# The second attention's edge list in rows of eight tiles, each with one span of 128 nodes

## The chip, the core and the metric

The kernel runs on one core of a Trainium2 chip. The time is the device time of one launch in microseconds (us), median of the runs shown. Names used below: PE is TensorE (matmuls; PEld its weight loads), DVE is VectorE, ACT is ScalarE, POOL is GpSimd, which here issues the gathers, SP is the engine whose queue starts most other transfers. SBUF is the on-chip memory, PSUM the small memory in eight banks that PE writes its products to.

## What is computed

A graph of 6250 nodes with 256 features goes through four steps, each added to its input: a graph attention over 206,250 edges, a mixture of eight experts, a weighted sum over the edges, and a second attention over another list of 131,072 edges, whose result picks two of four experts per node. The change is about the second attention. Cut to what matters:

```python
def second(x, src, dst):                   # x: 6250 x 256, 131072 edges
    h = (x @ W_gat).reshape(M, 4, 4)       # 4 heads, 4 experts
    e = leaky_relu(a_src[src] + a_dst[dst], 0.2)     # a_src, a_dst: sums of h * att
    ee = exp(e - segment_max(e, dst)[dst])
    alpha = ee / (segment_sum(ee, dst)[dst] + 1e-16)
    agg = segment_sum(h[src] * alpha[:, :, None], dst).reshape(M, 16) + b_gat
    scores = layernorm(agg).reshape(M, 4, 4).mean(1)
    topk_s, topk_i = top_k(scores, 2)
    w = softmax(topk_s)
    out = sum over e of where(topk_i == e, w, 0).sum(-1) * (gelu(x @ W1[e] + b1[e]) @ W2[e] + b2[e])
    return x + out
```

(A loop edge from each node to itself is part of both attentions; the kernel adds it apart from the lists.)

## The kernel before

One program, four stages, one after the other: the first attention (0 to about 2700 us), the experts with the sort of the second edge list beside them (to about 3700), the weighted sum (to about 6255), and the second attention (to the end of the span).

**Streams.** Both attentions run over an edge list sorted by destination, cut into *tiles* of 128 edges. A `Stream` (class at line 963) says which nodes a tile may meet. The destination of an edge at position p is close to p divided by the mean number of edges per node (`ratio`, 16 for the second list); `slack` is the largest deviation of ratio x destination from the position that the plan allows, and a check at run time (`check_stream`) chooses between the fast path described here and a slow one. Without groups (the second list, `s1`, line 1972), `window(b)` gives for each block b of 128 nodes the tiles that can hold edges into it: 16 tiles and 5 on each side for the slack of 640, so neighbouring windows overlap by ten tiles. With groups (the first list, `s0`, groups of 16 tiles), each group gets one *span* of 128 nodes that holds all that its tiles can meet. Spans don't begin at multiples of 128; `parts_of(b)` lists the spans that touch block b. `windows(t0, n)` lists the windows or spans that the tiles t0 to t0+n-1 meet.

**The loop.** `gat_stream` (1191 to 1449) does an attention. It works on *pieces* of Q = 8 tiles, in *batches* of B = 32 tiles (four pieces). The second list has 787 tiles, 99 pieces. The order of instructions on every engine is written out by hand (`manual_schedule`, the loop from 1405): engines take their queues strictly in this order, and step s_ issues

- `gathers(s_)`: eight indirect DMAs on POOL (1260) that fetch the source rows into `g` (nine buffers; the buffer of piece p comes free when `messages(p - 9)` of DVE is done),
- `load(s_+2)` on SP: `db` (destinations, 1244), once per batch `kf` (1253), and for a grouped stream `nbw`, the node part of one span (1249),
- `scores(s_-2)`: `node_parts` on PE multiplies the turned one-hot matrix `ot` of each tile by the node part (1281), into the PSUM tile `pd`; DVE sums its three terms (`nd`, 1290) and makes the scores (`z`, `Z`, 1292 to 1296); ACT copies edges of `Z` (1298, 1300),
- `move_sums` (grouped streams only, 1389): see below,
- `turned_hots(s_-1)` on DVE: `ot` (1270), one instruction for each window that the piece meets,
- `sums(s_-7)` on PE, the first two tiles (1363), and once per batch `turn_scores` (PE 1306, `zt`) and `greatest` (DVE scans `R`, `M`, 1312 and 1315),
- `one_hots(s_-6)` on DVE: `oh` (1152), one instruction for each window, comparing `ips` (node numbers, in PSUM) with the destinations,
- the rest of `sums`, which adds oh x messages to `acc`, one PSUM accumulator for each window,
- once per batch `turn_back` (PE 1323 and 1324, ACT exponentials 1328 and 1332, DVE products with `il` 1333),
- `keep_sums` (grouped only, ACT 1376), `done` for blocks whose sums are complete (in the second attention the DVE row `a` at 1781 and what follows it),
- `messages(s_-6)` on DVE: scaling (1340) and, in the second attention, splitting into three bf16 terms (1345, 1347).

`beside()` is called several times per step and issues other work: in the second attention first what is left of the second experts (PE 1714 and 1725, ACT 1719 and 1730, whose `y_d` stores go through SP), later the weighted additions to X (DVE 1813).

Without groups, `acc` of window b is already the sum of block b. With groups, `keep_sums` copies the finished sum of a span from PSUM to SBUF (`kept`), and in the next step `move_sums` adds it into the blocks that it touches (`bacc`), by a matmul with an identity matrix read at an offset (`shift_to`, `wide`).

PSUM: `place_iota` puts `ips` into a bank of its own, and `pd` has another. The node part in three bf16 terms, `NB`, stays in SBUF for an ungrouped stream; for a grouped one it is written to DRAM once (1221) and read back per span.

Of the kernel before, what the change touches and what calls it, by code (L numbers as in the profile page):

```python
# [20 lines left out]
F32 = mybir.dt.float32  # L21
# [11 lines left out]
P = 128  # L33
# [2 lines left out]
CH = 7  # L36
PAD = 30000
SLACK0 = 1024
SLACK1 = 640
GROUP0 = 16  # L40


def n_tiles(edges, nt):
# [28 lines left out]
def tile_kernel(ctx, tc, src_ins, out):  # L72
# [592 lines left out]
    I = src_ins  # L665
# [294 lines left out]
    Q = 8  # L960
# [172 lines left out]

    B = 32

    def place_iota(pp):

        t = pp.tile([P, 2 * P], F32, name="ips")
        nc.scalar.copy(t[:, :P], iota)
        nc.vector.tensor_scalar(t[:, P:], iota, float(P), None, op0=OP.add)  # L1140
        return t
# [49 lines left out]
    def gat_stream(s, H, CD, si, il, dl, tab, NI, early, done, parts=1, beside=None, pe=None):  # L1191
# [8 lines left out]
        W = DH + 2 * H  # L1200
        T = s.T
        ND = 2 * H
# [3 lines left out]
        with ExitStack() as st:  # L1206
# [5 lines left out]
            with tc.tile_pool(name="split", bufs=1) as sp:  # L1212
                NB = (sp if s.group else gp).tile([P, NT, 3, ND], BF, name="NB")
# [7 lines left out]
                    nc.sync.dma_start(nb_d.rearrange("(t p) d -> p t d", p=P), NB.rearrange("p t s d -> p t (s d)"))  # L1221
            mp = pool("gw", 2)
            pp = pool("gp", 1, space=PSUM)
            ips = place_iota(pp)
            piece, Z, acc, turned, hots, dbs, kfs, ps, ended = {}, {}, {}, {}, {}, {}, {}, {}, []
            items, split = {}, {}
            beside = beside or (lambda: False)

            def span(q):
                return q * Q, min(Q, T - q * Q)  # L1230
# [42 lines left out]

            def node_parts(q):
                t0, n = span(q)
                pd = pp.tile([P, Q, 3, ND], F32, name="pd", bufs=1)
                bl = turned.pop(q)
                for j in range(n):
                    use = [(b, o, t0 + j - a) for b, a, m, o in bl if a <= t0 + j < a + m]
                    for k, (b, o, i) in enumerate(use):  # L1280
                        nc.tensor.matmul(pd[:, j].rearrange("p s d -> p (s d)"), o[:, i * P:(i + 1) * P],
                                         nbw[b] if s.group else NB[:, b].rearrange("p s d -> p (s d)"),
                                         start=(k == 0), stop=(k == len(use) - 1))
                return pd
# [24 lines left out]
            def greatest(i, zt):  # L1309
                kf = kfs.pop(i)  # L1310
                R = mp.tile([P, 3 * P], F32, name="R")
                nc.vector.tensor_tensor_scan(R, kf[:, :3 * P], zt.rearrange("p k e -> p (k e)"), 0.0,  # L1312
                                             op0=OP.mult, op1=OP.max)
                M = mp.tile([P, 2 * P], F32, name="M")
                nc.vector.tensor_tensor_scan(M[:, ::-1], kf[:, 3 * P:P:-1], R[:, 3 * P - 1:P - 1:-1], 0.0,
                                             op0=OP.mult, op1=OP.max)
                d = mp.tile([P, P], F32, name="d")
                nc.vector.tensor_sub(d, zt[:, 1], M[:, :P])
                return d, M
# [51 lines left out]
            def keep_sums():  # L1371

                while ended:
                    i = ended.pop(0)
                    t = mp.tile([P, W], F32, name="kept", bufs=2)
                    nc.scalar.copy(t, acc.pop(i).rearrange("p s w -> p (s w)"))
                    moved.append((i, t))

# [16 lines left out]
            with tc.manual_schedule():  # L1395
# [9 lines left out]
                while s_ < last or later:  # L1405
# [10 lines left out]
                    if 0 <= k < npiece:  # L1416
                        scores(k, node_parts(k))
# [8 lines left out]
                    if batch:  # L1426
                        zt = turn_scores(i)
                        d, M = greatest(i, zt)
# [8 lines left out]
                    if s.group:  # L1437
                        keep_sums()
                        while ready:
                            b = ready.pop(0)  # L1440
                            follow(done(b, sums_of.pop(b), items.pop(b), mp))
# [9 lines left out]
    NB = 13  # L1451
# [293 lines left out]
    def layer1_fast(s1, si, dl1, il1, HN, tab_1, y_d, rest):  # L1745
# [4 lines left out]
        with tc.tile_pool(name="g1f", bufs=1) as g1, tc.tile_pool(name="f1w", bufs=2) as fp:  # L1750
# [75 lines left out]
            def beside():  # L1826
                if not rest() and work:
                    work.pop(0)()
                return bool(work)

            gat_stream(s1, H1, C1, si, il, dl, tab_1, NI, early, done, parts=3, beside=beside)

    moves = {}

    def fast(flag_s0, last_d, dl_d):
# [11 lines left out]
        with tc.tile_pool(name="gat0f", bufs=1) as g0:  # L1847
# [4 lines left out]
            with tc.tile_pool(name="rows", bufs=1) as p:  # L1852
                sr = load_rows(p, I["src"], s0.edges, C, I32, "sr")
                sf = p.tile([P, C, P], F32, name="sf")
                t = p.tile([P, C, P], F32, name="tt")
# [109 lines left out]
            with tc.tile_pool(name="f0h", bufs=1) as hp, tc.tile_pool(name="mix_ps", bufs=1, space=PSUM) as xp:  # L1965
                mix = xp.tile([P, 4 * P], F32, name="mix")
                par = head.params(hp)
                gat_stream(s0, H0, C0, si, il, dl, tab, NI, early, done, beside=lambda: next(par, True) is None,
                           pe=mix[:, :P].rearrange("p (b h) -> p b h", h=H0))


        s1 = Stream("s1", I["L1_ffn_edge_index"].shape[1], SLACK1, 1 << NB)
        C1s = s1.C
        si1 = dram.tile([P, C1s * P], I32, name="si1")
        dl1 = dram.tile([P, C1s * P], F32, name="dl1")
# [214 lines left out]
    for a, b in x_rows(x_in):  # L2190
        nc.scalar.dma_start(b, a)
    s0 = Stream("s0", I["src"].shape[0], SLACK0, N, GROUP0, True)
    last_d = dram.tile([P, s0.C, P], F32, name="last_d")
# [4 lines left out]
    with tc.If(v == 1) as cmp:  # L2198
        fast(s0, last_d, dl_d)
# [25 lines left out]
```

## Time and profile before

| what | value |
|---|---|
| three runs | 7765.84, 7773.18, 7774.26 us; median 7773.18 |
| profiled execution | 7783.37 us, its span 7781.5 us |
| granted PE clock, mean of the span | 0.717 |
| busy in the span | DVE 57%, POOL 53%, PE 49%, PEld 37%, ACT 15% |

By stage, busy us of each engine:

| stretch, us | PE | PEld | DVE | ACT | POOL | clock |
|---|---|---|---|---|---|---|
| 0 to 2700 | 1341.84 | 1034.21 | 1404.18 | 329.47 | 1544.64 | 0.73 |
| 2700 to 3700 | 876.16 | 756.89 | 470.24 | 250.03 | 252.15 | 0.94 |
| 3700 to 6255 | 1343.84 | 905.36 | 1705.19 | 471.84 | 1537.45 | 0.73 |
| 6255 to 7782 | 265.22 | 204.71 | 885.31 | 109.77 | 761.83 | 0.53 |

How to read what follows. A row of instructions gives the line, the engine, the operation, the output and inputs by their names in the program, the sizes (partitions x elements), the count, then busy us and mean ns of one, then the engine's idle time just before them and what ended most of it. A row of the timeline begins with its start and its duration in us; in brackets stands how long the engine had been idle before it and what released it. "remote" there is a release that the profile can't put down to a row, "issue" a time in which the engine waited for nothing that the profile shows. The ends of matmuls are modelled from their issue. Releasers are inferred.

### The profile page before, as it was taken

To read this page: it belongs to the slowest core of one execution; us is meant where nothing else is said; L and a number is where in the kernel's file an instruction comes from. 1 tells how busy PE (TensorE), PEld (TensorE's weight loads), DVE (VectorE), ACT (ScalarE), POOL (GpSimd) and SP (SyncE) were. 2 spreads that over 40 slices of the span, in tenths; PEclk is the share of its full clock that TensorE was granted. 3 is DMA by queue.
4 is the path that set the end of the run, shared out by engine and by line. 5 is a ranking of instruction groups with operands and counts; after the bars stand their busy time and mean duration, and the time that the engine had idled before them with its cause. 6 is when DMAs were issued, how large, how long until landed. Compare 5 with 4: busy or idle time off the path is not lost. (4 is left out here: it accounts for less than half of the span.)

```text
span 7781.5 us, 62325 instructions
## 1 busy us (share of the span) xinstructions
PE 3827.1 (49%) x17463; PEld 2901.2 (37%) x17463; DVE 4464.9 (57%) x10655; ACT 1161.1 (15%) x2758; POOL 4096.1 (53%) x4320
## 2 busy tenths in 40 slices
PE   3345545555445599996135555655555651111111
PEld 2234434444334378885023333433343431111111
DVE  4345555555555673443566666776676615665666
ACT  2011111111111112321001222212221210000000
POOL 0666666666666322321566666666566445555552
PEclk9667777777777799998557777777777875555555
DMA  4444444444444245565433333333333212222221
GB/s 124 119 114 119 113 117 120 117 119 118 115 114 120 73 163 190 184 228 167 139 89 99 98 103 100 101 102 102 95 100 101 80 43 52 45 48 52 50 50 41
DMA packets 496232, 821.82 MB, mean 106 GB/s; under 512 B 143344, under 2 KB 315587, under 8 KB 495842
## 3 DMA queue, kind: packets, MB, share of 16 engines
q0 software_dynamic: 190880, 462.26, 22.4%
q1 hardware_dynamic: 292326, 343.79, 14.5%
q10 hardware_dynamic: 12668, 11.68, 0.5%
q8 instruction: 141, 2.31, 0.1%
q14 instruction: 217, 1.78, 0.1%
HBM read 743.27 MB, written 77.29 MB: 105 GB/s over the span
## 5 line engine op out<-in xcount | busy, mean ns | idle before, releaser
L234 POOL DMA_INDIRECT g<-tab_ef,si x1616 | 1537.3, 951 | 995.4 <-issue 557.9
L1260 POOL DMA_INDIRECT g<-tab,si x1612 | 1539.6, 955 | 924.5 <-issue 577.4
L2028 DVE SCALAR_TENSOR_TENSOR run<-g,wab,run 128x256 f32<-128x256 f32 x2626 | 1264.9, 488 | 551.0 <-remote 179.2
L1260 POOL DMA_INDIRECT g<-tab_1f,si1s x787 | 761.8, 968 | 666.3 <-issue 587.1
L1363 PE MATMUL acc<-g,oh 128*128 128x264 f32 x3224 | 981.8, 465 | 174.6 <-issue 105.7
L1363 PEld LDWEIGHTS acc<-g,oh 128*128 128x128 f32 x3224 | 747.6, 238 | 365.0 <-issue 127.7
L1290 DVE TENSOR_REDUCE nd<-pd 128x64 f32<-128x192 f32 (+1 forms) x301 | 105.8, 352 | 1138.1 <-remote 914.2
L1714 PE MATMUL pf<-xt,w 128*128 128x512 f32 (+1 forms) x832 | 479.7, 715 | 474.9 <-issue 163.3
L2142 PE MATMUL acc<-run,oh 128*128 128x256 f32 x808 | 295.2, 500 | 628.3 <-DVE oh L2032 261.6
L1725 PE MATMUL pf<-w,h 128*128 128x256 f32 x1568 | 410.6, 412 | 183.1 <-ACT y L1730 80.9
L2142 PEld LDWEIGHTS acc<-run,oh 128*128 128x128 f32 x808 | 192.9, 251 | 730.4 <-issue 444.8
L1340 DVE TENSOR_TENSOR g<-g,mix 128x2048 f32<-128x2048 f32 x202 | 457.5, 2265 | 0.0
L1714 PEld LDWEIGHTS pf<-xt,w 128*128 128x128 f32 x832 | 179.7, 235 | 665.2 <-issue 321.6
L1363 PE MATMUL acc<-s,oh 128*128 128x72 bf16 x1267 | 96.6, 251 | 665.9 <-DVE s L1345 491.1
L1725 PEld LDWEIGHTS pf<-w,h 128*128 128x128 f32 x1568 | 316.3, 207 | 253.4 <-ACT y L1730 87.4
L1306 PE MATMUL zt<-ident,Z 128*128 128x128 f32 x228 | 76.6, 400 | 676.7 <-issue 380.2
L630 PE MATMUL ph<-xe,w 128*128 128x256 f32 x1792 | 405.4, 383 | 4.7 <-DVE xe L618 4.7
L643 PE MATMUL py<-w,h 128*128 128x256 f32 x1792 | 397.3, 379 | 0.0
L630 PEld LDWEIGHTS ph<-xe,w 128*128 128x128 f32 x1792 | 341.2, 192 | 51.4 <-DVE xe L618 5.7
L643 PEld LDWEIGHTS py<-w,h 128*128 128x128 f32 x1792 | 335.6, 190 | 43.1
L1363 PEld LDWEIGHTS <-oh 128*128 128x128 bf16 x1267 | 90.2, 133 | 669.9 <-issue 576.9
L606 POOL DMA_INDIRECT xg<-tab_x,gi x112 | 125.8, 1123 | 387.6 <-PE pt L615 313.1
(506 smaller groups left out, 5933.3 us busy)
## 6 DMA issues: line engine op xcount, KB each, us to landing
w<-in_L_ffn_W SPq DMA_DIRECT2D x112, 1024.0 KB
db<-s_d SPq DMA_DIRECT2D x299, 256.0 KB
g<-tab_ef,si POOLq DMA_INDIRECT x1616
g<-tab,si POOLq DMA_INDIRECT x1612
y_d<-y SPq DMA_DIRECT2D x196, 128.0 KB
yb<-y_d SPq DMA_DIRECT2D x49, 512.0 KB
g<-tab_1f,si1s POOLq DMA_INDIRECT x787
yy<-tab_y SPq DMA_DIRECT2D x7, 1792.0 KB
```

The costliest lines, as they stand in the source:

```text
L234: nc.gpsimd.indirect_dma_start(out=dst, out_offset=None, in_=table, in_offset=bass.IndirectOffsetOnAxis(ap=si[:, t:t + 1], axis=0))
L606: nc.gpsimd.indirect_dma_start(out=xg[:, i, :], out_offset=None, in_=tab_x, in_offset=bass.IndirectOffsetOnAxis(ap=gi[:, 2 * j + i:2 * j + ...
L630: nc.tensor.matmul(ph, w1[:, k, f * P:(f + 1) * P], xe[:, k, :], start=(k == 0), stop=(k == KD - 1))
L643: nc.tensor.matmul(py, hs[f][:, i * P:(i + 1) * P], w2[:, f, :], start=(f == 0), stop=(f == FC - 1))
L1260: nc.gpsimd.indirect_dma_start(out=g[:, j, :DH + H], out_offset=None, in_=tab, in_offset=bass.IndirectOffsetOnAxis(ap=si[:, t0 + j:t0 + j ...
L1290: nc.vector.tensor_reduce(nd[:, :n], pd[:, :n].rearrange("p j s d -> p j d s"), AX.X, OP.add)
L1340: nc.vector.tensor_mul(gh, gh, ps[0][:, o:o + n, :, None].to_broadcast([P, n, H, CD]))
L1363: nc.tensor.matmul(acc[b].rearrange("p s w -> p (s w)"), oh[:, t - a], m_, start=(t == lo), stop=(t == hi))
L1714: nc.tensor.matmul(ph[:, :n], w1[:, e, k, f * P:(f + 1) * P], xts[g][:, k, :n], start=(k == 0), stop=(k == KD - 1))
L1725: nc.tensor.matmul(py[:, :D], hs[g, e, f][:, j * P:(j + 1) * P], w2[:, e, f, :], start=(f == 0), stop=(f == FC - 1))
L2028: nc.vector.scalar_tensor_tensor(at[:, i] if j < Q - 1 else r[i], g[:, j, :], w, at[:, i], op0=OP.mult, op1=OP.add)
L2142: nc.tensor.matmul(acc[i], oh[:, k], r[k], start=(q % 2 == 0 and k == 0), stop=(last and k == 1))
```

## The change

The second list is made a grouped stream with groups of eight tiles, and its slack goes from 640 to 496. A group is then one piece: 1024 edges, 64 nodes by the ratio, and 62 more for the slack on both sides, within one span of 128. Spans of neighbouring pieces begin 64 nodes apart. So:

- every piece meets one span; `ot` and `oh` are made once per piece, and each of its tiles has one weight load and matmul in `pd` and one in `acc`;
- the list has 786 tiles, 99 pieces as before;
- `NB` of the second attention is held only for a while, written to DRAM, and read back per span (`nbw`);
- the sums of a span are copied by ACT (`kept`, now `parts * W` = 72 wide in the second attention, W = 264 as before in the first) and added to the blocks by the shifted identity; a block is put together from four spans.

In `gat_stream`, which both attentions run, `ips` and `pd` come to lie in one PSUM tile of one bank, `bank`.

```diff
-SLACK1 = 640
+SLACK1 = 496
 GROUP0 = 16
+GROUP1 = 8
...
-    def place_iota(pp):
-
-        t = pp.tile([P, 2 * P], F32, name="ips")
+    def place_iota(t):
+
         nc.scalar.copy(t[:, :P], iota)
         nc.vector.tensor_scalar(t[:, P:], iota, float(P), None, op0=OP.add)
         return t
...
             pp = pool("gp", 1, space=PSUM)
-            ips = place_iota(pp)
+
+            bank = pp.tile([P, 4 * P], F32, name="bank", bufs=1)
+            ips = place_iota(bank[:, :2 * P])
+            pd = bank[:, 2 * P:2 * P + Q * 3 * ND].rearrange("p (j s d) -> p j s d", j=Q, s=3)
...
             def node_parts(q):
                 t0, n = span(q)
-                pd = pp.tile([P, Q, 3, ND], F32, name="pd", bufs=1)
                 bl = turned.pop(q)
...
                 while ended:
                     i = ended.pop(0)
-                    t = mp.tile([P, W], F32, name="kept", bufs=2)
+                    t = mp.tile([P, parts * W], F32, name="kept", bufs=2)
                     nc.scalar.copy(t, acc.pop(i).rearrange("p s w -> p (s w)"))
                     moved.append((i, t))
...
-        s1 = Stream("s1", I["L1_ffn_edge_index"].shape[1], SLACK1, 1 << NB)
+        s1 = Stream("s1", I["L1_ffn_edge_index"].shape[1], SLACK1, 1 << NB, GROUP1)
```

## The prediction, made before the changed kernel was run

> **What bounds the kernel now.** The change acts on one stage, the second attention, which begins with its first gathers at about 6261 us and runs to the end of the span. I read the slices first: from slice 33 on PE falls to 1 tenth, while DVE stands at 6 and POOL at 5, so no engine is full. Then busy time per stretch, in columns PE, PEld, DVE, ACT, POOL, granted clock, DMA share, GB/s:
>
> ```profile
> 6520.00:6636.00 116.00, 15.58 (x218) 12.48 (x218) 71.84 (x217) 6.81 (x22) 61.35 (x64) 0.50 0.20 49
> 6868.00:6984.00 116.00, 15.58 (x218) 12.47 (x218) 71.66 (x216) 6.81 (x22) 62.07 (x64) 0.50 0.21 49
> 7448.00:7564.00 116.00, 15.58 (x218) 12.49 (x218) 73.71 (x220) 6.81 (x22) 63.90 (x66) 0.50 0.21 49
> ```
>
> All stretches from 6404 to 7680 look so: 64 gathers (eight pieces) in close to 115.5 us (64 gathers began between 6856.06 and 6971.5), 14.4 us per piece. Is it POOL? A gather is 0.95 us and the next follows after 0.30, so 64 need 80 us. POOL has 35 us of slack per eight pieces; its waits are buffers that come back late. DVE's busy 72 us are 78 with the roughly 30 ns between its 216 instructions. The other 37.8 us are waits, by the groups of 6856 to 6971.5: nd 21.2, R 10.4, the il product 6.2. What do they wait for?
>
> ```profile
> 6901.85 0.65 PEld L1281 LDWEIGHTS <-ot 128*128 128x128 bf16 x13
> 6902.06 0.54 PE L1281 MATMUL pd<-NB,ot 128*128 128x24 bf16 x13
> 6902.42 0.10 PEld L1363 LDWEIGHTS <-oh 128*128 128x128 bf16 x1
> ...
> 6910.24 0.94 PE L1363 MATMUL acc<-s,oh 128*128 128x72 bf16 x13 [7.63 <-DVE s L1345]
> ...
> 6925.41 0.36 DVE L1290 TENSOR_REDUCE nd<-pd 128x64 f32<-128x192 f32 x1 [15.22 <-remote]
> 6925.81 0.19 DVE L1292 TENSOR_TENSOR z<-g,nd 128x32 f32<-128x32 f32 x1
> ...
> 6926.81 0.20 PE L1281 MATMUL pd<-NB,ot 128*128 128x24 bf16 x1 [15.63 <-DVE ot L1270]
> 6927.07 1.95 DVE L1152 TENSOR_TENSOR oh<-ips,dl1s 128x1024 bf16<-128x1024 f32 x2
> ...
> 6932.95 0.95 POOL L1260 DMA_INDIRECT g<-tab_1f,si1s  x1 [10.98 <-issue]
> ```
>
> nd reads only pd. z, the first reader of the gathered rows, then starts without a wait, so the 15.22 us were not for a gather. The matmuls of pd are listed (with modelled ends) at 6902, yet the reader starts 23 us later: at such places PE delivers late. The same is seen at 7591.50 (pd listed) and 7614.12 (nd, 15.08). It comes about once per batch of four pieces; in the first attention too, whose pieces already meet one window (nd at 1535.88, 8.75). Its cause is in no view I have. So the stage is bound by DVE's work in series with late deliveries of PE.
>
> **The change, part by part.** 787 tiles are 99 pieces; today a piece meets two windows, 8 + 5 tiles.
>
> ```profile
> L1152 DVE TENSOR_TENSOR oh<-ips,dl1s 128x1024 bf16<-128x1024 f32 x98 | 118.8, 1212 | 0.0
> L1152 DVE TENSOR_TENSOR oh<-ips,dl1s 128x640 bf16<-128x640 f32 x96 | 77.8, 811 | 0.0
> L1270 DVE TENSOR_SCALAR ot<-db,s_nid 128x1024 bf16<-128x1024 int16 x98 | 48.2, 491 | 4.3 <-DMA db<-s_d 4.3
> L1270 DVE TENSOR_SCALAR ot<-db,s_nid 128x640 bf16<-128x640 int16 x96 | 38.9, 405 | 0.0
> L1281 PE MATMUL pd<-NB,ot 128*128 128x24 bf16 x1267 | 63.1, 184 | 270.7 <-DVE ot L1270 214.7 <-issue 38.6 <-remote 14.8
> L1363 PE MATMUL acc<-s,oh 128*128 128x72 bf16 x1267 | 96.6, 251 | 665.9 <-DVE s L1345 491.1 <-DVE g L1347 95.3 <-issue 79.5
> ```
>
> *DVE, removed:* the second of each pair, 96 x (811 + 405 ns) = 116.7 us of busy time. Pairs overlap in part: by starts, two oh take 1.86 us (6927.07 to 6928.93) against 1.13 for one in the first attention (1507.44 to 1508.57), two ot about 0.78 against 0.46. That is 1.05 us per piece, 8.4 per eight; nothing lies over it.
>
> *PE, removed:* 5 of 13 pairs of weight load and matmul per piece in pd and in acc. When PE is on time this is worth nothing (15.6 of 116 us busy). When it is late it counts: 23.3 us for 13 pairs of pd would be 14.3 for 8. DVE then has 8.1 - 1.05 = 7 us of work over it, so that wait falls from 15.2 to about 7.3. A batch also has a smaller wait at R, behind the 13 sums; sums fall to 8, but two shift matmuls join them. Two batches: 2 x 7.9 less at nd, and 10.4 x 3/13 = 2.4 at R, 18 together. The bounds: nothing, if lateness is a fixed stretch of time that only slides, and 18. I take 10, nearer the middle because the first attention, with 8 pairs, still shows such waits (80.7 us at nd in 500 us).
>
> *PE and ACT, added:* each of 49 blocks is put together from 4 spans, 196 fp32 shift matmuls. The row of the same line in the first attention has 647 ns (264 wide), the 128-wide fp32 transposition 447; for 72 columns I take 0.4 us, 2 x 0.4 per piece on an engine that idles 100 of 116 us: nothing, and 13 us over the stage per 0.13 us that would show. ACT copies 99 sums (379 ns at 264 wide) beside 6.8 us of busy per 116: nothing. If that copy waits for late sums, Z's copies queue behind it on ACT, and turn_scores behind those, but PE itself is then the cause. The block's first DVE row, a, read acc straight after its sums; now it reads bacc, filled earlier in the step, and follows one step later. Only the last step of the stage is longer for it: +3 us.
>
> *SP, added:* NB goes to DRAM once and returns as 99 rows of 48-byte lines, 0.38 us of issue each on a queue with one db per piece: hidden, two pieces ahead. At the start it is not: the first nbw load must await NB's write (issued 177.8 in the first attention, first nbw at 189.6, so 12 us), and behind it in SP's queue stand db, kf and the FFN's y stores, whose landing lets ACT go on. Between 0 and 15 us; until 6404 the FFN's rest sets the pace anyway (POOL waits 53.5 us for ACT y), so what delays it counts: +10.
>
> *Slack 640 to 496, one tile fewer:* one gather, 1.25 us, in POOL's slack. The span of a piece is 64 nodes and 2 x 496/16 = 62 for the slack, so it fits 128. In the inputs 16 x destination minus position in the sorted list lies between -345 and 39, so the fast branch holds.
>
> *One bank for ips and pd, in both attentions.* By the trace, pd of the next piece runs inside oh: matmuls from 6926.81 and 6927.20, oh from 6927.07 to 6929. The Trainium skill, "PSUM — Partial Sum Buffer", section "PSUM bank collisions raise a hardware error", says that two engines may not use one bank on the same partitions at once, disjoint columns included, and that semaphores must guard it "by bank × quadrant (by bank is the simple version), not by address". This rule speaks against the change: by address pd stays where the row has it and costs 0; by bank it moves behind oh, and with no cover that is oh's 1.2 us at each of 301 pieces of both attentions, 361 us. No row here shows two engines on one bank. Cover is there: after oh come the messages (L1340 0.28 + 3 x 0.28 + 2 x 0.36 = 1.8 us here, one of 2.27 us in the first attention), and eight pairs of pd need 0.35 (1510.87 there, already behind oh). So on-time steps pay nothing; where PE is late it starts up to 1.2 us later, about 25 batches here: between 0 and 30, and I take +8.
>
> **The sum.** A period of eight pieces: 115.5 - 8.4 - 10 = 97, 12.1 us per piece. The first attention, with one window per piece, has 333 gathers in 500 us, 12.0 per piece, which agrees. Over 1274 us (6404 to 7678): 1274 x 18.4/115.5 = 203. Less 10 (start), 8 (bank), 3 (end): 182. The profiled execution is 7783.37 us (span 7781.5), 0.13% over the median of the runs, 7773.18; it would become 7601, the median 7591. What is late next: still PE's deliveries; POOL (80 of 97) comes close.
>
> **Rivals.**
> (1) *Only DVE's work goes*; the lateness is a fixed time per batch, or the shift matmuls fill what the pairs leave. For it: the first attention shows as much of it with 8 pairs. Against: fewer pairs lie ahead of nd. 1274 x 8.4/115.5 = 93, less 21: 72, giving 7701.
> (2) *POOL becomes the bound.* The lateness hangs on the second window and vanishes: 82 us per eight pieces, 1274 x 33.5/115.5 = 370, less 21: 7424. Against it: the first attention.
> (3) *Slower: the bank order is exposed.* pd must wait for oh and DVE for pd, in 301 pieces: 7591 + 361 = 7952 if never covered. It decides from 182/301 = 0.6 us per piece, when PE reaches pd more than 1.8 us after oh's end, as it may in the first attention, where PE is half busy with sums. Against: there pd follows the sums today already.
> (4) *The change doesn't act* (slow branch): excluded by the inputs.
>
> **Chances.** Forecast 0.55, its own range 7540 to 7650; rival 1 0.20; rival 2 0.08; rival 3 0.12; costs that just cancel the gain 0.05. A difference below 0.2% (15.5 us) can't be told from none. Faster: 0.55 + 0.20 + 0.08 = 0.83; within 0.05; slower 0.12. The range 7500 to 7715 takes in the forecast with its open costs (stall 0 to 18, start, bank) and rival 1, and leaves out rivals 2 and 3.
>
> **What would show it.** oh and ot once per piece, 1.21 and 0.49 us; pd and acc x786; 64 gathers in about 97 us; nd waits below 21 per eight pieces. If nd and R still wait 31, rival 1; if POOL shows no waits for buffers, rival 2. If in the first attention nd waits for pd just after each oh, and that stage is longer than before, the bank order costs. A wait of nbw for NB's write shows at 6260 to 6290.

## The result and the profile after

The changed kernel takes 7820.91 us (16 runs, 7781.04 to 7856.26) where the kernel before takes 7773.72 (16 runs, 7754.3 to 7796.24): ratio 1.005, interval 1.0035 to 1.0065. It is slower by half a percent. The profiled execution took 7818.24 us, its span 7816.4.

What the change removes is gone, by the groups of the second attention in the changed kernel (same columns as before):

```profile
L1152 DVE TENSOR_TENSOR oh<-bank,dl1s 128x1024 bf16<-128x1024 f32 x98 | 118.9, 1213 | 0.0
L1391 PE MATMUL bacc<-kept,wide 128*128 128x72 f32 x390 | 109.3, 434 | 384.8 <-ACT kept L1378 255.5 <-issue 123.1 <-ACT g L1334 6.0
L1365 PE MATMUL acc<-s,oh 128*128 128x72 bf16 x786 | 68.9, 250 | 248.6 <-DVE s L1347 230.3 <-issue 18.3
L1273 DVE TENSOR_SCALAR ot<-db,s_nid 128x1024 bf16<-128x1024 int16 x98 | 47.0, 480 | 14.8 <-DMA db<-s_d 14.8
L1283 PE MATMUL bank<-nbw,ot 128*128 128x24 bf16 x786 | 36.4, 181 | 415.9 <-DVE oh L1152 364.6 <-issue 48.3 <-DMA kf<-s_keep 1.5
L1292 DVE TENSOR_REDUCE nd<-bank 128x64 f32<-128x192 f32 x98 | 34.6, 353 | 639.5 <-remote 598.9 <-PE bank L1283 35.2 <-issue 4.7
```

oh and ot run once per piece, pd and acc have 786 matmuls. A shift matmul leaves two records here, so there are 390 (of 392) where I wrote 196. And nd now waits 639.5 us in the stage, against 372.6 before. Busy time by stretch, in the changed kernel:

```profile
6868.00:6984.00 116.00, 19.27 (x170) 15.62 (x170) 63.03 (x199) 8.14 (x30) 58.41 (x62) 0.50 0.22 49
7448.00:7564.00 116.00, 18.64 (x162) 15.12 (x163) 62.92 (x199) 8.14 (x30) 58.43 (x62) 0.50 0.23 49
```

DVE works 63 us of 116 where it worked 72, yet POOL now issues fewer gathers in the same time (62, not 64). So DVE's saved time became waiting. To compare kernels I take from each trace the time from the 13th to the 93rd nd of the second attention, a tenth of which is the mean of eight pieces, and DVE's gaps of over 0.3 us in it. The stage is counted from its first row on DVE (NI1f, at 6255.55 before and at 6239.66 after):

| | before | after |
|---|---|---|
| eight pieces, us | 114.9 | 117.3 |
| DVE's gaps in them, us | 37.1 | 46.5 |
| first row of the stage to its first nd, us | 104.8 | 117.9 |
| the same to the 13th nd, us | 238.1 | 261.0 |
| 93rd nd to the end, us | 138.3 | 142.7 |
| whole second attention, us | 1525.7 | 1576.6 |

The mean depends a little on where the 80 pieces begin: from the 9th to the 18th nd it is 113.0 to 115.8 us before and 117.3 to 120.4 after. The waits have also moved. Between 6400 and 7680, R waited 78.6 us and the il product 60.4 before, 9.8 and 4.3 after, while nd went from 247.9 to 494.6: nearly all of DVE's waiting now stands at nd.

The timeline of the changed kernel shows where nd waits (cut to the gathers that begin after a stop of POOL, to nd's long waits, and to PE and ACT around the first of them):

```profile
6913.77 0.94 POOL L1263 DMA_INDIRECT g<-tab_1f,si1s  x1 [10.42 <-issue]
...
6925.58 0.36 PE L1283 MATMUL bank<-nbw,ot 128*128 128x24 bf16 x8 [1.83 <-DVE oh L1152]
...
6935.07 0.22 ACT L1378 COPY kept<-acc 128x72 f32<-128x72 f32 x1 [14.98 <-remote]
...
6947.65 0.36 DVE L1292 TENSOR_REDUCE nd<-bank 128x64 f32<-128x192 f32 x1 [20.12 <-remote]
...
6954.10 0.94 POOL L1263 DMA_INDIRECT g<-tab_1f,si1s  x1 [10.49 <-issue]
...
6999.19 0.36 DVE L1292 TENSOR_REDUCE nd<-bank 128x64 f32<-128x192 f32 x1 [20.82 <-remote]
...
7012.54 0.98 POOL L1263 DMA_INDIRECT g<-tab_1f,si1s  x1 [18.65 <-issue]
```

pd is listed at 6925.58 and arrives 22 us later; kept, a copy on idle ACT, waits for late sums in the same stretch. What I had not asked of the trace before is what POOL does then. It issues gathers in unbroken rows, one each 1.25 us: here 24 from 6913.77 to 6943.7, and 32 from 6954.10 to 6993.9. Each wait of nd of 20 us lies in such a row, begins 13 us or more after its start, and ends 3 to 5 us after the end of its last gather. The kernel before has a similar picture. Its stops of POOL:

```profile
6856.06 1.03 POOL L1260 DMA_INDIRECT g<-tab_1f,si1s  x1 [8.98 <-issue]
...
6869.92 0.99 POOL L1260 DMA_INDIRECT g<-tab_1f,si1s  x1 [4.06 <-issue]
...
6891.54 1.04 POOL L1260 DMA_INDIRECT g<-tab_1f,si1s  x1 [11.34 <-issue]
```

The last of these begins a row of 24 gathers that ends at 6922.0, and the wait of 15.22 us shown in the prediction ended at 6925.41. Before, the rows per eight pieces are 8, 8, 24, 24; after, 8, 24, 32. The rows of eight have no long wait in either. Not all of it fits so well: before, the waits of 14 to 15 us end 2 to 3 us after the end of a row, but those of 9 to 10 us end some 8 us ahead of their row's last gather. And the trace alone doesn't say which causes which, since POOL also stops because a waiting DVE returns no buffers.

### The profile page after: what moved, and what is told of

Same layout as the page of the kernel before. It is cut to its first block, busy times and chain, and to the rows that moved or that the text cites. A ratio compares the mean times of both kernels' runs of the same rounds, so it can differ in the third digit from the quotient of the medians.

```text
span 7816.4 us, 61328 instructions
## 1 busy us (share of the span) xinstructions
PE 3902.1 (50%) x16891; PEld 2949.7 (38%) x16891; DVE 4361.4 (56%) x10463; ACT 1177.1 (15%) x2857; POOL 4079.8 (52%) x4278
## 3 DMA queue, kind: packets, MB, share of 16 engines
q0 software_dynamic: 190848, 462.25, 22.3%
## 5 line engine op out<-in xcount | busy, mean ns | idle before, releaser
L1292 DVE TENSOR_REDUCE nd<-bank 128x64 f32<-128x192 f32 (+1 forms) x301 | 106.0, 352 | 1374.4 <-remote 1132.4
L1391 PE MATMUL bacc<-kept,wide 128*128 128x264 f32 (+1 forms) x790 | 286.6, 511 | 485.7 <-ACT kept L1378 304.8
L1391 PEld LDWEIGHTS bacc<-kept,wide 128*128 128x128 f32 x790 | 189.8, 297 | 512.7 <-ACT kept L1378 309.7
L1283 PE MATMUL bank<-nbw,ot 128*128 128x24 bf16 x2398 | 109.5, 178 | 494.8 <-DVE oh L1152 371.5
```

The costliest lines, as they stand in the source:

```text
L1391: nc.tensor.matmul(sums_of[b].rearrange("p s w -> p (s w)"), shift_to(s, i, b), t, start=(i == of[0]), stop=(i == of[-1]))
```

## The experiments

The theories at the start: A, the shared bank's order makes pd late; B, the rows of gathers make PE late; C, the shift matmuls do.

**Two banks.** ips and pd apart again (in the second attention ips goes to SBUF).

```diff
-            bank = pp.tile([P, 4 * P], F32, name="bank", bufs=1)
-            ips = place_iota(bank[:, :2 * P])
-            pd = bank[:, 2 * P:2 * P + Q * 3 * ND].rearrange("p (j s d) -> p j s d", j=Q, s=3)
+            ips = place_iota((pp if parts == 1 else gp).tile([P, 2 * P], F32, name="ips", bufs=1))
+            pd = pp.tile([P, Q, 3, ND], F32, name="pd", bufs=1)
```

> The change without its shared bank: in the first attention ips and pd have a PSUM bank each again, in the second ips lies in SBUF and pd alone in its bank, so pd need not wait for oh. Theory A (the bank's order: pd begins only after oh and so arrives late): the waits of nd fall back to well below the 50 us per eight pieces of the changed kernel, eight pieces of the second attention take 100 us or less, and the time is below 7690 us. Theory B (PE delivers late while POOL issues gathers in an unbroken row, whatever the bank): two waits of nd of about 20 us per eight pieces stay, eight pieces take 115 to 120 us, and the time stays within 25 us of the changed kernel's 7821.

Measured: 7782.01 us, ratio to the kernel before 1.0002 (0.9985 to 1.0019), so 39 us less than the changed kernel in the runs of the result, and 35 less than the run with seven buffers below, on the same chip and with the shared bank. But eight pieces take 116.8 us (115.3 to 116.8 by other starts) and the gaps are 46.5, as in the changed kernel. Theory A doesn't explain the waits; the bank is a cost beside them. In the two profiles the second attention is 24 us shorter (1552.4), 17 of them ahead of the 13th nd (one profile of each). As ips also moved to SBUF, those 39 us are of both together.

**Seven buffers** for the gathered rows.

```diff
-                g = piece[q] = mp.tile([P, Q, W], F32, name="g", bufs=9)
+                g = piece[q] = mp.tile([P, Q, W], F32, name="g", bufs=9 if parts == 1 else 7)
```

> The change with seven buffers in place of nine for the gathered rows of the second attention, so that POOL is held closer behind DVE and its rows of gathers are shorter. Theory A: no gain, since the bank's order is as before: 119 us per eight pieces or more, time 7815 to 7860. Theory B: rows of 24 and 32 gathers become rows of 8 to 16, the late stretches of PE, which begin about 10 us into a row, become shorter: eight pieces in less than 112 us, time below 7760.

Measured: 7816.82 us, ratio 1.005 (1.0022 to 1.0078), eight pieces 119.3 us, rows still 8, 24, 32. Fewer buffers don't shorten the rows, so this says nothing of what a shorter row would do; my guess that buffers set the rows fell.

**No gathers.** Each piece loads the first rows of the table by a plain transfer, in place of the rows that its edges name.

```diff
+                if parts > 1:
+                    nc.sync.dma_start(g[:, :n, :DH + H], tab[:n * P].rearrange("(p n) d -> p n d", p=P))
+                    return
                 for j in range(n):
                     nc.gpsimd.indirect_dma_start(
```

> The change with the 786 gathers of the second attention left out: each piece loads the same number of bytes by one plain transfer from SP's queue instead, always the first rows of the table. Theory A: PE still waits for oh and nd for pd: the waits of nd of about 20 us stay, two per eight pieces. Theory B: with no gathers on POOL no wait of nd is above 8 us, and eight pieces take what DVE has to do, 62 us and its small waits: 66 to 80 us, so that the second attention is 400 us shorter or more.

Measured: 7197.5 us, eight pieces 71.0 us, gaps 1.2. Its group of nd and a stretch:

```profile
L1295 DVE TENSOR_REDUCE nd<-bank 128x64 f32<-128x192 f32 x98 | 34.4, 351 | 49.1 <-PE bank L1286 49.0
6868.00:6984.00 116.00, 27.75 (x252) 22.23 (x251) 101.89 (x324) 13.22 (x46) 0.00 (x0) 0.50 0.32 75
```

With the same matmuls, the same bank and the same clock of 0.50, no wait of nd for "remote" is left, and DVE is busy 102 of 116 us. So without gathers PE is on time. The edit takes out POOL's work and the packets of its queue together; which of the two acts isn't separated. The list of waits still has pd waiting for oh, 239.0 us in 80 waits between 6400 and 7100: that wait is long and costs nothing.

**One shift of four.** Three of the four additions that put a block together are left out.

```diff
                         of = s.parts_of(b)
+                        if parts > 1:
+                            of = of[-1:]
```

> The change with three of the four shifted additions of each block left out (only the last span's is made), 98 records of shift matmuls in place of 390. Theory C (the shift matmuls are what makes PE late, between pd and the sums of every piece): the two long waits of nd per eight pieces fall from 20 to below 14 us and eight pieces take less than 108 us. Theory B: PE carries 17 instead of 20 pairs per piece in the same rows of gathers, so at most a sixth of the waits goes: 112 to 119 us. Theory A: 119 us.

Measured: 7804.04 us (one run), eight pieces 117.7 us, gaps 47.0. Theory C falls.

**Pauses.** POOL gets other work between gathers: four or two memsets of 128x1024 after each piece, or one of 128x256 after each gather.

```diff
                         in_offset=bass.IndirectOffsetOnAxis(ap=si[:, t0 + j:t0 + j + 1], axis=0))
+                if parts > 1:
+                    for _ in range(4):
+                        nc.gpsimd.memset(rest_[:, :1024], 0.0)
```

> The change with four memsets of 128x1024 on POOL after the eight gathers of each piece of the second attention (about 1.0 us each, from the row of 248 elements at 0.295 us): POOL issues eight gathers in 10 us and then none for about 4 us. Theory B1 (it is the unbroken row of gathers that makes PE late, and a pause of some us ends it): no wait of nd above 8 us is left, the waits of DVE fall from 46 to below 15 us per eight pieces, and POOL's 8 x 14 us set the pace: 110 to 115 us per eight pieces. Theory B2 (it is the number of gathers per time): waits shrink in proportion, about as much time as POOL spends in memsets: 112 to 120 us with waits of 25 us or more. Theory B3 (any work of POOL makes PE late, memsets too): waits grow, 125 us or more.

> As the one with four memsets, with two: a pause of about 2 us after each eight gathers, POOL 12 us per piece. Theory B1: if 2 us are enough to end the lateness, 96 to 102 us per eight pieces and a time near 7640; if they are not, waits of nd of 20 us stay and eight pieces take 117 us or more. Theory B2: waits of 35 us or more, 115 to 120 us. Theory B3: 120 us or more.

> The change with one memset of 128x256 (about 0.3 us) on POOL after every gather of the second attention: about as much time between gathers as with two memsets per piece, but spread, so that the row of gathers has no pause of more than 1 us. Theory B1: waits of nd of about 20 us stay, as the row is unbroken: 117 to 130 us per eight pieces. Theory B2: the same as with two memsets of 1 us per piece, whatever that is. Theory B3: 120 us or more.

| | time, us | eight pieces | gaps, and for what |
|---|---|---|---|
| four memsets | 7739.2 | 113.2 | 38.7, z |
| two memsets | 7525.05 | 97.0 | 22.3, z |
| one per gather | 7552.12 | 94.3 | 22.3, z |

The last two are clearly faster than the kernel before on the same chip (7772.37), although POOL has more to do. Each is one run; the 33 us by which the first is below it are less than the 43 us over which sixteen runs of the kernel before spread there (7762.4 to 7805.3). The long waits of nd are gone in all three; what is left is z, the first reader of the gathered rows, so POOL sets the pace (two memsets, stretch 6400 to 7300, waits by line). The view puts z's waits down to "issue" there; with four memsets it names the gathers, 231.4 us in the same stretch.

```profile
PE bank L1287 <- DVE oh L1152: 358.2, 56, 15.5
...
DVE z L1298 <- issue: 201.9, 39, 7.7
```

The one with a memset per gather has no pause after each eight: its gathers follow at 1.45 us each in rows of up to 424, and PE is on time, by its group of nd:

```profile
L1295 DVE TENSOR_REDUCE nd<-bank 128x64 f32<-128x192 f32 x98 | 33.7, 344 | 52.7 <-PE pf L1730 24.5 <-PE bank L1286 8.3 <-PE pf L1719 7.5
```

So it is not the unbroken row (B1) but the gathers per time (B2), with a sharper edge than B2 had it: the waits don't shrink in proportion, they are gone.

**Very short memsets**, 128x8, after each piece or each gather.

> The change with one memset of 128x8 (about 0.1 us) on POOL after the eight gathers of each piece of the second attention. Theory R (PE is late when gathers come faster than about one in 1.3 us for long; what helped was the time between them): the rate stays 1.25 us, so two waits of nd of 20 us stay, 117 us per eight pieces. Theory I (an ordinary POOL instruction between gathers ends the lateness, however short): no wait of nd above 8 us, POOL's 64 x 1.25 plus eight memsets set the pace: 80 to 86 us per eight pieces, time near 7400.

> The change with one memset of 128x8 after every gather of the second attention. With 256 elements it was 1.47 us per gather. Theory R: 1.30 to 1.35 us per gather is near the old rate: waits of nd of 10 us or more stay and eight pieces take 100 us or more. Theory I: no such waits, 82 to 88 us per eight pieces.

Measured: 7811.73 and 7846.14 us (before: 7798.54 on that chip); 117.6 and 117.7 us for eight pieces; gaps 46.8 and 47.0. The memset of 128x8 fits into the 0.3 us between two gathers: their spacing stays 1.25 and 1.26 us, and nd waits as ever (memset per piece, stretch 6400 to 7600):

```profile
POOL g L1264 <- issue: 547.7, 618, 18.7
DVE nd L1295 <- remote: 449.8, 27, 30.6
```

So another kind of POOL instruction in between is not what helps; of what was tried, the time between the gathers is left.

**The kernel before with a memset of 128x256 per gather.**

> The kernel before the change, with one memset of 128x256 after every gather of the second attention, as in the run of the changed kernel that took 94.3 us per eight pieces. If the lateness is what joins all these kernels, the waits of nd and R go here too (37 to below 5 us per eight pieces); DVE has 78 us of work, so POOL's 64 x 1.47 = 94 us set the pace, 94 to 98 us per eight pieces, and the time lies within 40 us of the changed kernel with the same memsets (7552). If the lateness needs the change's one-span pieces, it stays: 115 us or more.

Measured: 7477.68 us against 7798.54 on that chip. Eight pieces take 94.8 us, gaps 16.2, nearly all of z; the whole second attention 1242.3 us, and the changed kernel with the same memsets 1247.4. The 74 us between the two times, more than the 40 that I allowed, lie elsewhere: the second attention began at 6233 us here and at 6303 there, and over the profiles of this kind of chip at anything from 6227 to 6303.

**The kernel before without gathers**, the same edit as above.

> The kernel before the change with the gathers of the second attention left out in the same way as in the changed kernel that took 71.0 us per eight pieces (one plain transfer per piece from SP's queue, always the first rows of the table). If DVE's part of the prediction is right (8.4 us per eight pieces, hidden by nothing once PE is on time), eight pieces take 79 to 80 us here. If the second window costs PE time too, 85 us or more; if DVE's removed rows were worth nothing, 71.

Measured: eight pieces 78.5 us, gaps 1.7. Against 71.0 in the changed kernel, taken on another chip, DVE's part is worth 7.5 us per eight pieces (8.4 predicted). Its time, 6417.61 us, came with a surprise: the kernel before took 6482.17 us on this chip (9 runs, 6479.07 to 6491.48), not 7770. Three more runs went there and were to find how short the pauses may be:

> The change with one memset of 128x128 (about 0.17 us) after every gather of the second attention: between 128x8, which left the spacing at 1.26 us and the lateness as it was, and 128x256, which made it 1.45 us and ended it. Theory R (time between gathers): somewhere between; if the spacing is 1.32 us or more and the lateness is over, eight pieces take 84 to 90 us; if it is not, waits of nd stay and eight pieces take 105 us or more.

> The kernel before the change with one memset of 128x256 (bf16) on POOL after every gather of all three gather stages. If the lateness of PE holds back the first attention and the weighted sum as it does the second attention, all three stages shorten: the first attention goes from 12.0 to about 11.7 us per piece at POOL's pace, the second to 94 us per eight pieces: time 7400 to 7480. If those two stages are bound otherwise, only the second attention gains: 7470 to 7560. If a bf16 memset is too short to spread the gathers, no gain: 7770.

> The kernel before the change with one memset of 128x1024 after the eight gathers of each piece of the second attention, a pause of 1 us in place of 2. Theory R: if the mean spacing decides (11 us per piece, 1.38 us per gather), the lateness is over and eight pieces take 88 to 92 us; if the pause must last 2 us, waits of nd of 10 us or more stay: 105 us or more.

| | time, us | eight pieces | spacing of gathers, us |
|---|---|---|---|
| change, 128x128 per gather | 6566.81 | 88.4 | 1.34 |
| before, 128x256 per gather, all stages | 7275.68 | 94.4 | 1.44 |
| before, 128x1024 per piece | 6547.98 | 88.1 | 1.25, then the pause |

Here PE was never late, with or without a pause (no wait of nd over 8 us from the 13th nd to the 93rd in any of these profiles; the kernel before takes 6482), so they can't tell how short a pause would do on the other chips. All that they show is POOL's added time: the one in all stages is 12% slower than the kernel before (1.1222, 1.1207 to 1.1237).

**The changed kernel on such a chip**, unedited, and the kernel before with four memsets of 128x256 bf16 per piece in all three gather stages.

> The changed kernel as it is, once more, beside the kernel before on the chip that this call gets. In the call before this one the kernel before took 6482 us where it had taken 7762 to 7805 on the two chips until then, and no wait of nd was left in any run there: PE was on time. If this call's chip is one of the late kind (kernel before near 7770), the changed kernel takes 7790 to 7850 again. If it is one where PE is on time (kernel before near 6480), eight pieces take POOL's 64 x 1.25 = 80 to 83 us in both kernels, and what is left of the change is its slower start and end, 10 to 20 us: 6485 to 6510, ratio 1.000 to 1.005.

> The kernel before the change with four memsets of 128x256 bf16 (about 1.2 us together) on POOL after each eight gathers of all three gather stages, 1.40 us per gather on the mean in place of 1.25. On a chip of the late kind: by theory R, if 1.40 us on the mean is enough, no long waits of nd or R are left and all three stages run at about POOL's pace, 11.2 us per piece: 6800 to 7100 us; if the pause is too short, waits stay and the time is above 7500. On a chip where PE is on time: POOL's added time only, 6600 to 6800, slower than the kernel before.

Measured on another chip where the kernel before takes 6482.12 us: the changed kernel 6479.52, ratio 0.9996 (0.9987 to 1.0005), no difference, and a little below the 6485 to 6510 that I expected. Its stretches, and its groups of nd and z:

```profile
5600.00:5716.00 116.00, 30.20 (x267) 24.13 (x266) 86.36 (x273) 10.89 (x44) 88.07 (x92) 0.50 0.33 72
5800.00:5916.00 116.00, 23.18 (x203) 18.30 (x202) 93.52 (x293) 11.14 (x37) 88.26 (x92) 0.50 0.30 66
L1292 DVE TENSOR_REDUCE nd<-bank 128x64 f32<-128x192 f32 x98 | 34.4, 351 | 51.2 <-PE bank L1283 51.2
L1294 DVE TENSOR_TENSOR z<-g,nd 128x32 f32<-128x32 f32 x98 | 18.9, 193 | 122.6 <-issue 112.3 <-DMA g<-tab_1f,si1s 7.3 <-DVE nd L1292 0.2
```

92 gathers in 116 us are 1.26 us each: POOL never stops, one row of 642 gathers in the steady part, and nd has no wait for "remote". Eight pieces take 81.6 us, POOL's time. The paused kernel took 7264.58 us (ratio 1.1203, 1.1185 to 1.1222), its eight pieces 95.0. That is far above my 6600 to 6800: four memsets take 1.44 us in its trace, not 1.2, and the 783 us are 1.56 for each of the 503 pieces of the three stages.

**Half the pause, and the whole once more.**

> The kernel before the change with two memsets of 128x256 bf16 on POOL after each eight gathers of all three gather stages, a pause of about 1 us, 1.37 us per gather on the mean. On a chip of the late kind (kernel before near 7770): if 1 us is enough, no long waits are left and the stages run at about 11 us per piece, 6850 to 6980 us; if not, long waits of nd and R stay and the time is above 7400. On a chip where PE is on time: POOL's added time only, about half of the 783 us that four memsets cost: 6840 to 6900.

> The kernel before the change with four memsets after each eight gathers of all three gather stages, once more. Where PE is on time it took 7264.6 us, POOL setting the pace. On a chip of the late kind: by theory R the pause ends the lateness in all three stages, and the time is the same as there, 7255 to 7290, 6 to 7% below the kernel before on the same chip; if the first attention and the weighted sum are late for another reason, 7350 or more.

Again the kernel before took 6482.01 us: 7016.72 (1.0823, 1.0804 to 1.0843) and 7263.39 us (1.1202, 1.1182 to 1.1222). The first lies above my 6840 to 6900, but its edit did more than it should: it also halved the calls of `beside` in the experts' stage (line 649, four to two), so more of what runs beside them follows them. From the first attention's last nd to the weighted sum's first gather it took 1209 us, and 1080 and 1078 with four memsets and line 649 as it was. Less these 130 us it would take about 6887, an estimate, within the range. Neither could meet its question: whether pauses in all three stages end the lateness on the other chips was not tried there.

## Why the prediction was wrong

**The step that failed** is the one on PE's removed work: "The bounds: nothing, if lateness is a fixed stretch of time that only slides, and 18. I take 10". I took PE's lateness for something that a pair of weight load and matmul pays, so that fewer pairs would pay less. It hangs on POOL's gathers: on the chips where it shows, PE is late in long rows of gathers at 1.25 us each, and on time when they come at 1.45, or in eights with about 2 us between. The gaps of DVE went not from 37 to 27 but to 46.5, outside both my bounds: the 7.5 us that DVE lost in work, and 2 more, came back as waiting. That a DVE with less to do returns buffers sooner, so that POOL stops three times in eight pieces in place of four and its rows grow from 24 to 32, fits the rows of the trace but is argued, not isolated.

**DVE's part** was right in size where nothing hides it: 78.5 - 71.0 = 7.5 us per eight pieces, 8.4 predicted. It was not on the path: where PE is late the waits take it back, where PE is on time POOL does.

**The sum**: eight pieces 97 predicted, 117.3 measured. The check against the first attention ("12.0 per piece, which agrees") compared with a stage under the same lateness; where PE is on time that stage takes 10.1 us per piece ((2233 - 193)/201, from its first and last nd). The count was off as well: between 1500 and 2000 the trace has 329 gathers, not 333, and the whole stage took 12.3 us per piece.

**The shared bank** was sized 0 to 30, +8; with ips in SBUF and pd apart the kernel is 39 us faster. By the two ratios to the kernel before it is 0.48%, 37 us with some 18 either way (an estimate from the two intervals), so at my upper end or above. It isn't exposed at each piece (rival 3, +361): where PE is on time the messages hide it, as argued. Without gathers, nd waits for PE 49.1 us in the whole stage with the shared bank, and 49.2 in the kernel before, whose pd has its own. The order by bank that the Trainium skill asks for ("PSUM — Partial Sum Buffer", section "PSUM bank collisions raise a hardware error") shows in the trace as a wait of pd for oh, 1.83 us in the row at 6925.58; no run here shows the two engines on one bank without it. The bank decides the sign on the chips where PE is late: with two banks the change is level. Why it costs more than nothing where PE is late (pd enters the late stretch later) is argued only.

**The start** was +10; the first nd came 13.1 us later, with two banks too (118.0), so that is NB's way through DRAM and not the bank. Where PE is on time it is 40.6 against 27.0 (in the kernel before with a memset per piece), and in the kernel before with a memset per gather, on a chip of the late kind, 27.2. The stage opens with a row of 72 gathers, and before the change nd's first wait, 95.8 us, lasts until 10 us after the last of them began. So most of the 104.8 us ahead of the first nd are PE's lateness as well, and not only "the FFN's rest" that I read there. **The end**, +3, measured +4.4. **Shift matmuls**, nothing: right (one of four: 117.7), though their records are twice as many.

**Rival 2** (POOL the bound) is what happens where PE is on time, 81.6 us against my 82. But there the kernel before has POOL's bound as well, so its gain of 349 us is none. **Rival 1** took the waits as fixed; they grew.

**A better version.** On the chips where PE is late, memsets on POOL in the second attention alone bring the kernel before from 7798.54 to 7477.68 and the changed one to 7525.05 (one run each), the fastest there. On the others they only add to POOL's time (12% in all three stages with four memsets per piece; 8% with two, some 2% of it from line 649), and there neither kernel was beaten.

## What to carry to other kernels

When an engine waits for a result whose instructions were listed long before, ask what all the other engines do in that stretch, also those that it doesn't depend on; here the rows of the gathers pointed to the cause, and they stood in the trace before the change. Before work is taken off an engine, ask which limit comes next on the path and whether it is fixed: DVE's 7.5 us per eight pieces were real and were worth nothing, behind PE's lateness on one chip and POOL's pace on the other. Where a wait has no cause in any view, its price under the change is open to both sides, growth too. And measure on a second chip: the same two kernels differ by half a percent on one kind and not at all on the other.

## What the runs showed of the hardware

The kernel before took 7754 to 7805 us in the runs of the result and on the two chips of the first experiments, and 6477 to 6492 on the two chips of the later ones, with the same program. On the first kind, long rows of gathers (mostly 24 and more) at 1.25 us each made PE late and 1.45 did not; on the other kind 642 gathers at 1.25 us in a row did nothing to PE. The granted clock is no difference: 0.50 in the stretches of both kinds. No chip was seen both ways, and all late runs came before all others, so whether it is the chip or something beside the program at that time stays open. So does the path by which gathers reach PE: the last packet of a gather ended 2.1 us after its issue (median), inside nd's long waits as outside. ACT's kept and DVE's nd took 216 and 353 ns on the mean in the changed kernel where PE is late, 216 and 351 where it is on time.

Rows of DVE became longer beside memsets on POOL: ot went from 480 to 743 ns on the mean beside two memsets of 128x1024 per piece, and to 555 beside 128x256 per gather.
